# Layer 0's routing beside its attention, row transfers in pairs, layer 1's projection one period later, and VectorE's order there left to the scheduler

## The chip, the cores and the metric

The kernel runs on one core of one Trainium2 chip. The metric is device time in microseconds, the median of several runs: 1300.3 us for the kernel before (three runs, 1290.47 to 1302.03). Besides these there is one profiled execution, from which every detail below comes; its own time is given with the profile.

A core has engines that run independently and meet only through semaphores: TensorE (PE, with PEld for the loading of weights), VectorE (DVE), ScalarE (ACT), GpSimd (POOL) and SyncE (SP), whose queue issues most DMAs. [...]

## The reference

Four layers work on x of shape 4 x 512 x 128 (four batches of 512 tokens) with a context ctx of 4 x 154 x 128. Each layer adds an attention on the context and then a mixture of 8 experts, both on a layer norm of x:

```
x = x + attention_l(layernorm(x), ctx)
x = x + experts_l(layernorm(x))
```

Layer 0's attention is a similarity with softmax (H is the normalized x, C the context of the same batch):

```
Sim  = (H @ w1)[:, :, None] + (C @ w2)[:, None, :] + (H * w3) @ C.T + b
hq   = softmax(Sim, over C) @ C
hc   = softmax(max of Sim over C, over H) @ H         # one row per batch
out  = concat[H, hq, H * hq, H * hc] @ W_qv + b_qv
```

Layer 1's attention has 16 heads of 8 columns; queries, keys and values come from 8 x 8 matrices shared by all heads, there is a mask, and the output goes through Wo and bo. Layers 2 and 3 have 16 heads of 64 columns. The experts of layers 0, 2 and 3 take the best two of 8 experts for each token, those of layer 1 the best one with a capacity; layer 0's expert is a gated one with two up matrices, the others have one.

## The kernel before

**Tiling.** x stays in SBUF as four tiles x[b] of 128 x 4 x 128, one for each batch; a group of 128 tokens is a "tile" i of a batch. The experts of a layer run in two halves: half 0 holds the tokens of batches 0 and 1, half 1 those of batches 2 and 3. `route` (a generator, run in steps between its `yield`s) norms its two batches, computes the gate logits, finds the best experts, the rank of every token within its expert and from these a slot number (`su`, line 716). Scatters by indirect DMA from POOL's queue (line 721, one for 128 tokens and one choice) bring the normed tokens into blocks of 128 in DRAM, `buf`; `experts` loads these blocks (line 838, after all scatters of the half), runs up and down products, and stores `ybuf`; `gather` fetches the rows back by indirect DMA (line 939), and `combine` adds them to x (line 957). Scatters and gathers are first put into a list, `rows_due`; `row_transfers(n, behind)` issues the next n of them, tied with a wait to the instruction `behind`, or all at once without.

**Layer 0's attention** (`layer0_setup`, lines 960 to 1060). `prepare(b)` norms batch b, transposes it (xnT), and computes Sim for the four tiles in PSUM: a matmul with rhs1 (which holds w1 and w3 * C) and a second one, with w2b as its weights, that adds C @ w2 to every row (lines 979 and 980); VectorE copies to SBUF and adds b (line 983), takes maxima, and ScalarE exponentiates. `tile_of` divides by the sums, transposes the probabilities (pm and pt, copied by `evac`, which alternates between VectorE and ScalarE), multiplies by the context (hq), forms hc with its denominator by 4 + 4 matmuls with one column (lines 1034 and 1036), builds three feature tiles ft, and accumulates four products for each tile (line 1049). `attend_first` (from line 1261) runs `prepare(0)`, then tile(0), prepare(1), tile(1), prepare(2) and so on; layer 0's `route` for half 0 starts before prepare(3), goes six steps, and is finished after tile 3. After it, `row_transfers()` issues all its scatters, and `experts` begins. The buffer of sim exists once. No order is written by hand in layer 0; the framework's scheduler orders every engine's instructions by their place in the program and by a simulated timeline.

**Layer 1's attention** (`attend_all`, from line 1277). 16 periods, one for each tile of tokens, under `manual_schedule` for PE, ACT and DVE: on these engines instructions stay in the order in which the code writes them. A period overlaps the tile `new` (scores, maxima, exponentials) with the tile `old` before it (transposes, product with V, projection) and the first scores of `nxt`. The 16 heads are done in three groups g of 6, 6 and 4: `score(g)` on PE into a PSUM tile "sc" (two buffers), `most(g)` on VectorE (nm, line 291), `exp(g)` on ScalarE (line 305). `short` copies the last 26 columns of each head's probabilities; `inverse` takes the reciprocal of the sums; `replicate` transposes these (line 332), copies them (rT, line 334) and spreads them over 128 rows through DRAM by two DMAs of SP's queue (rd and rep, lines 339 and 340). `turn_ends`, `turn(0..3)` transpose old's probabilities into PSUM tiles "tr" (two buffers, also used by `replicate` and `project`); `take_ends`, `take(n)` copy these to SBUF on VectorE (line 261), and `take` also issues two row transfers; `by_v_ends`, `by_v(n)` multiply with V (line 405); `scaled` multiplies by rep (line 412); `project` (line 422) and `residual` (lines 1164 and 1165) add to x. `middle` and `after` run steps of `route` or of combining beside it, `parts` prepares the next batch (norm, values, keys and queries) in four portions. Before, a period of layer 1 (`narrow_period`, lines 432 to 485) is in this order:

```
new.score(1)  old.turn_ends  old.turn(0)  new.most(1)  new.exp(0)  new.exp(1)
old.take_ends  old.take(0)  old.by_v_ends  old.turn(1)  old.take(1)  new.score(2)
old.turn(2)  old.by_v(0)  old.by_v(1)  new.most(2)  new.exp(2)  old.take(2)
old.turn(3)  old.by_v(2)  old.take(3)  old.by_v(3)  old.scaled(0)
middle  parts  nxt.score(0)  nxt.most(0)  new.short  new.inverse  queries
new.replicate  old.project  old.residual  after
```

Layers 2 and 3 use `wide_period`, which stays as it is apart from an argument.

**The head of the program.** SP's queue issues x[0] to x[3], the two parts of the context (lines 108, 112, 113), then nine small loads for the gates (lines 1225, 1229, 183), then layer 0's weights (w_sim at line 207, then b_sim, b_qv, wqv), the clearing of `buf`, and layer 0's down matrices.

Of the kernel before, what the change touches and what calls it, by code (L numbers as in the profile page):

```python
# [19 lines left out]
P = 128  # L20
# [6 lines left out]
E = 8  # L27
# [19 lines left out]
def tile_xattn_moe_stack(ctx: ExitStack, tc: tile.TileContext, a: dict, out: bass.AP):  # L47
# [33 lines left out]
    turn = [0]  # L81

    def evac(o, i, scale=None):

        turn[0] += 1
        if turn[0] % 2:
            if scale is None:
                nc.vector.tensor_copy(o, i)
            else:
                nc.vector.tensor_scalar(o, i, scale, None, ALU.mult)  # L90
        elif scale is None:
            nc.scalar.copy(o, i)
        else:
            nc.scalar.activation(o, i, AF.Copy, scale=scale)
# [10 lines left out]
    x = []  # L105
    for b in range(B):
        t = xpool.tile([P, NI, D], F32, tag=f"x{b}", name=f"x{b}")
        nc.sync.dma_start(t, x_in[b])
        x.append(t)
# [3 lines left out]
    nc.sync.dma_start(ctail, a["ctx_1024"][:, P:S2, :].rearrange("b k d -> k b d"))  # L113

# [89 lines left out]
    def columns(src, rows, name):  # L204

        t = p2.tile([rows, P], F32, tag="rows", name=f"{name}_r")
        nc.sync.dma_start(t, src)
# [224 lines left out]
    def narrow_period(new, old, nxt=None, middle=nothing, queries=nothing, parts=nothing, after=nothing):  # L432
# [9 lines left out]
        if old:  # L442
            old.turn_ends()
            old.turn(0)
        if new:
            new.most(1)
            new.exp(0)
            new.exp(1)
        if old:
            old.take_ends("v")  # L450
            old.take(0, "v")
            old.by_v_ends()
            old.turn(1)
            old.take(1, "v")
        if new:
            new.score(2)
        if old:
            old.turn(2)
            old.by_v(0)
            old.by_v(1)  # L460
        if new:
            new.most(2)
            new.exp(2)
        if old:
            old.take(2, "v")
            old.turn(3)
            old.by_v(2)
            old.take(3, "v")
# [3 lines left out]
        parts()  # L472
        if nxt:
            nxt.score(0)
            nxt.most(0)
# [4 lines left out]
        if new:  # L480
            new.replicate()
        if old:
            old.project()
            old.residual()
        after()

    def wide_period(new, old, nxt=None, middle=nothing, queries=nothing, parts=nothing, after=nothing):
# [472 lines left out]
    def layer0_setup():  # L960
        wsim = columns(a["L0_xattn_w_sim"].rearrange("(k p) -> k p", p=P), 3, "wsim")
# [437 lines left out]
```

## Time and profile before

| | |
|---|---|
| median of three runs | 1300.3 us (1290.47 to 1302.03) |
| profiled execution, its own time | 1392.9 us |
| its span, first to last instruction | 1390.8 us |
| mean granted clock of TensorE | 0.902 |
| busy in the span: PE, DVE, ACT, POOL | 1125.7, 736.2, 575.6, 252.9 us |
| layer 0: attention, and the way to its experts | 0 to 117.6 us |
| layer 0: experts | 117.6 to 270 us |
| layer 1: attention (exponentials 271.2 to 519.4) | 271 to 521 us |
| layer 1: experts | 523 to 613 us |
| layer 2: attention, experts | 614 to 850, 855 to 978 us |
| layer 3: attention, experts and end | 979 to 1226, 1230 to 1391 us |

A profiled execution is one execution with the profiler on; its times of single instructions are read against its own total, not against the median. In lines of a timeline the columns are start and duration in us, engine, line of the kernel, operation, output and inputs, shapes, and count; in brackets the idle time of the engine ahead of it and what ended it. "remote" means that the profile knows no releaser on this core.

### The profile page before, as it was taken

The numbers are of one execution on the slowest core, as the hardware profiler recorded it, in microseconds if no ns is written. First come the engines' busy times: TensorE is split into PE (matmuls) and PEld (weight loads), VectorE is DVE, ScalarE is ACT, GpSimd is POOL, SyncE is SP. The second block draws the span as 40 slices with busy tenths as digits, with TensorE's granted clock in tenths as the row PEclk, the third lists the DMA queues.
The fourth block names the chain that finished last, engine by engine and source line by source line (L and its number), as shares of the span: only waits on it lengthen the run. The fifth ranks groups of instructions, "written<-read, shape, count | busy, mean of one in ns | idle before, by whom it ended". The sixth has DMA issues, their size and how long they took to land.

```text
span 1390.8 us, 26946 instructions
## 1 busy us (share of the span) xinstructions
PE 1125.7 (81%) x9435; PEld 924.2 (66%) x9435; DVE 736.2 (53%) x2057; ACT 575.6 (41%) x2290; POOL 252.9 (18%) x281
## 2 busy tenths in 40 slices
PE   5876998976777689788999988657879999898881
PEld 3766997833344348776878767646668778787771
DVE  4563546546667655235667665314456667454442
ACT  1113333543454444355665554212545655432220
POOL 2031314031000101302000031332220000304224
PEclk8787999968998879999999999767999999899996
DMA  6014685611010215532212224442321112245652
GB/s 210 1 65 118 207 251 182 196 51 29 9 22 27 70 27 141 148 98 47 47 32 56 54 66 121 120 124 80 116 47 39 40 33 47 66 109 142 179 163 69
DMA packets 136995, 126.80 MB, mean 91 GB/s; under 512 B 13466, under 2 KB 116511, under 8 KB 136479
## 3 DMA queue, kind: packets, MB, share of 16 engines
q1 hardware_dynamic: 129695, 110.39, 28.6%
q0 software_dynamic: 7168, 14.69, 3.7%
q8 instruction: 77, 1.26, 0.4%
q14 instruction: 55, 0.45, 0.1%
HBM read 101.31 MB, written 23.72 MB: 90 GB/s over the span
## 4 chain that ended last, share of the span: by engine, by line
PE 36%; DVE 8%; issue 4%; ACT 4%; DMA 4%; another core or an unknown queue 3%; POOL 1%; SPq 1%; POOLq 0%; DVEq 0%; ACTq 0%
PE sc L875 5%; PE sc L608 5%; PE av L405 4%; PE av L906 4%; PE tr L368 4%; PE tr L422 4%; DMA w<-in_up 3%; ACT probs L305 2%; PE sc L593 2%; PE av L387 2%; DVE nm L291 2%; PE sc L557 1%; POOL yg L939 1%; DVE aT L412 1%
## 5 line engine op out<-in xcount | busy, mean ns | idle before, releaser
L305 ACT ACTIVATE probs<-sc,nm 128x154 f32<-128x154 f32 x768 | 287.0, 402 | 193.6 <-DVE nm L291 178.4
L875 PE MATMUL sc<-tokT,w 128*128 128x128 f32 x1528 | 214.6, 290 | 19.8 <-DMA w<-in_up 14.8
L875 PEld LDWEIGHTS sc<-tokT,w 128*128 128x128 f32 x1528 | 195.0, 202 | 31.0 <-DMA w<-in_up 11.1
L906 PE MATMUL av<-w,hT 128*128 x1160 | 179.2, 292 | 42.7 <-issue 19.2
L291 DVE TENSOR_REDUCE nm<-sc 128x6 f32<-128x924 f32 x144 | 143.2, 1010 | 100.7 <-PE sc L608 47.9
L906 PEld LDWEIGHTS av<-w,hT 128*128 128x128 f32 x1160 | 155.9, 201 | 53.9 <-issue 22.9
L305 ACT ACTIVATION_READ_ACCUMULATOR probs<-sc,nm 128x1 f32 x768 | 168.0, 219 | 0.0
L939 POOL DMA_INDIRECT yg<-ybuf,su x112 | 107.0, 956 | 295.5 <-DVE ys L914 67.1
L233 POOL TENSOR_TENSOR rstd<-ve,nhalf 128x4 f32<-128x4 f32 x32 | 33.1, 1034 | 652.4 <-DVE ve L231 544.4
L721 POOL DMA_INDIRECT buf<-xn,su x112 | 108.4, 968 | 184.0 <-DVE eb L744 78.7
L261 DVE COPY pT<-tr 128x512 f32<-128x512 f32 x160 | 107.3, 687 | 62.0 <-PE tr L368 48.6
L368 PE MATMUL tr<-ident,probs 128*128 128x128 f32 x768 | 123.9, 293 | 0.7 <-DVE rT L334 0.7
L405 PE MATMUL av<-pT,vm 128*64 128x128 f32 (+1 forms) x1536 | 104.5, 285 | 18.4 <-DVE pT L261 16.8
L368 PEld LDWEIGHTS tr<-ident,probs 128*128 128x128 f32 x768 | 88.0, 148 | 29.4 <-issue 14.5
L914 DVE COPY ys<-av 128x128 f32<-128x128 f32 x168 | 48.0, 286 | 111.2 <-PE av L906 73.4
L405 PEld LDWEIGHTS av<-pT,vm 128*64 128x64 f32 (+1 forms) x1536 | 65.2, 127 | 46.8 <-DVE pT L261 25.9
L891 ACT ACTIVATE eg<-sc,w 128x128 f32<-128x128 f32 x184 | 52.9, 370 | 89.2 <-PE sc L875 52.2
L608 PE MATMUL sc<-kT,qT 64*128 64x154 f32 x1024 | 85.1, 304 | 3.5 <-ACT probs L305 3.5
L895 DVE SCALAR_TENSOR_TENSOR hT<-sc,w,eg 128x128 f32<-128x128 f32 x184 | 55.9, 342 | 53.4 <-ACT eg L891 50.6
L608 PEld LDWEIGHTS sc<-kT,qT 64*128 64x128 f32 x1024 | 69.8, 186 | 14.5 <-issue 10.1
L593 PE MATMUL sc<-xnT,wq 128*128 128x128 f32 x512 | 70.8, 296 | 2.9 <-ACT probs L305 2.9
L593 PEld LDWEIGHTS sc<-xnT,wq 128*128 128x128 f32 x512 | 64.9, 206 | 8.2 <-issue 4.3
(252 smaller groups left out, 1504.8 us busy)
## 6 DMA issues: line engine op xcount, KB each, us to landing
w<-in_up SPq DMA_DIRECT2D x46, 516.0 KB
w<-in_up SPq DMA_DIRECT2D x76, 258.0 KB
rep<-rd SPq DMA_DIRECT2D x64, 256.0 KB
ybuf<-ys SPq DMA_DIRECT2D x168, 64.0 KB
tok<-buf SPq DMA_DIRECT2D x36, 256.0 KB
w<-in_down SPq DMA_DIRECT2D x3, 2048.0 KB
w<-in_up SPq DMA_DIRECT2D x46, 128.0 KB
buf<-zero SPq DMA_DIRECT2D x2, 1472.0 KB
```

The lines of the kernel that those rows point to most:

```text
L261: return nc.vector.tensor_copy(o, i)
L291: nc.vector.tensor_reduce(self.at.heads(self.nm, g, n), self.sc[g][:, :, 0 : n * S2].rearrange("p j (s k) -> p j s k", s=n), AX.X, ALU.max ...
L305: nc.scalar.activation(self.pr[:, h, :], self.sc[g][:, j, s * S2 : (s + 1) * S2], AF.Exp, bias=self.nm[:, h : h + 1], accum_out=self.rs[:, ...
L368: nc.tensor.transpose(q[:, t * P : (t + 1) * P], self.pr[:, h, 0:P], ident)
L405: nc.tensor.matmul(av[rows, cols], v, self.pT[n][:, t, :], start=False, stop=last)
L593: nc.tensor.matmul(sc[:, c // 4, c % 4 * P : (c % 4 + 1) * P], wq[:, c * P : (c + 1) * P], at.xnT[:, i * P : (i + 1) * P], start=True, sto ...
L608: nc.tensor.matmul(sc[:, j, s * S2 : (s + 1) * S2], at.qT[i][rows, c, :], at.kT[rows, c, :], start=True, stop=True)
L721: ins = nc.gpsimd.indirect_dma_start(out=buf[half], out_offset=bass.IndirectOffsetOnAxis(ap=su[:, t : t + 1], axis=0), in_=xns[t // NI][:, ...
L875: nc.tensor.matmul(dst, w[:, at : at + P], xT, start=True, stop=True)
L895: products.append(nc.vector.scalar_tensor_tensor(hT[:, fc, :], up, b0, g, ALU.add, ALU.mult))
L906: nc.tensor.matmul(y[:, 0:D], hT[:, fc, :], w2[:, bass.ds(e, 1), fc, :].rearrange("p o d -> p (o d)"), start=(fc == 0), stop=(fc == nf - 1),)
L939: ins = nc.gpsimd.indirect_dma_start(out=yg[:, t, :], out_offset=None, in_=ybuf[half], in_offset=bass.IndirectOffsetOnAxis(ap=su[:, t : t ...
```

## The change

It has four parts.

- **Head and layer 0's arithmetic.** w_sim's rows and the context are loaded before x[1] to x[3]; the gates' small loads move behind layer 0's weights. C @ w2 + b is computed once for all batches (`row`) and added by VectorE when it takes Sim from PSUM, in place of the second matmul. The denominator of hc comes from one matmul on ScalarE's accumulated sum `es`. H * hc @ W3 + H @ W0 becomes one product with wc = W3 * hc + W0, so that three products are left of four.
- **Layer 0's order.** `sim` gets two buffers; batches 0 and 1 are prepared first, then tile 0, prepare(2), tile 1, three steps of `route`, prepare(3), five more (up to the list of scatters), tile 2, a step, tile 3. Four instructions of each tile call `row_transfers(2, ...)`.
- **Layer 1's period.** The order is new (below); the sums' reciprocals are replicated in the period after, and the projection and residual of a tile come two periods after its scores (`older`). Keys and queries use PSUM tiles "tr" and "av" instead of "sc". Transposed tiles that `evac` copies go to VectorE alone (`busy`).
- **VectorE in layer 1** is taken out of the engines whose order the code sets; the scheduler draws it up.

```diff
+    x = [xpool.tile([P, NI, D], F32, tag=f"x{b}", name=f"x{b}") for b in range(B)]
+    nc.sync.dma_start(x[0], x_in[0])
+    sim_rows = p2.tile([3, P], F32, tag="rows", name="sim_rows")
+    nc.sync.dma_start(sim_rows, a["L0_xattn_w_sim"].rearrange("(k p) -> k p", p=P))
...
+    for b in range(1, B):
+        nc.sync.dma_start(x[b], x_in[b])
```

The period of layer 1:

```diff
         if new:
             new.score(1)
-        if old:
-            old.turn_ends()
-            old.turn(0)
-        if new:
             new.most(1)
             new.exp(0)
-            new.exp(1)
+        if older:
+            older.project()
+            older.residual()
         if old:
+            old.replicate()
+            old.turn_ends()
             old.take_ends("v")
+            old.turn(0)
             old.take(0, "v")
             old.by_v_ends()
             old.turn(1)
             old.take(1, "v")
+        parts()
         if new:
+            new.exp(1)
             new.score(2)
-        if old:
-            old.turn(2)
-            old.by_v(0)
-            old.by_v(1)
-        if new:
             new.most(2)
             new.exp(2)
         if old:
+            old.by_v(0)
+            old.turn(2)
             old.take(2, "v")
+            old.by_v(1)
+        if nxt:
+            nxt.score(0)
+            nxt.most(0)
+        if old:
             old.turn(3)
+            old.take(3, "v")
             old.by_v(2)
-            old.take(3, "v")
             old.by_v(3)
             old.scaled(0)
         middle()
-        parts()
-        if nxt:
-            nxt.score(0)
-            nxt.most(0)
         if new:
             new.short()
             new.inverse()
         queries()
-        if new:
-            new.replicate()
-        if old:
-            old.project()
-            old.residual()
         after()
...
-    ordered = {mybir.EngineType.PE, mybir.EngineType.Activation, mybir.EngineType.DVE}
+    ordered = {mybir.EngineType.PE, mybir.EngineType.Activation}
+    ordered_all = ordered | {mybir.EngineType.DVE}
...
+        busy[0] = layer == 1
+        with tc.manual_schedule(engines=ordered if layer == 1 else ordered_all):
```

Layer 0:

```diff
+        row = w1.tile([P, B, S2], F32, tag="wv", name="row")
+        sc = ps_sc()
+        for j in range(2):
+            nc.tensor.matmul(
+                sc[:, j, 0 : 2 * S2],
+                w2b,
+                ctxT[:, 2 * j : 2 * j + 2, :].rearrange("p b k -> p (b k)"),
+                start=True,
+                stop=True,
+            )
+        nc.vector.tensor_scalar(
+            row.rearrange("p (j b) k -> p j (b k)", j=2), sc[:, :, 0 : 2 * S2], bsim, None, ALU.add
+        )
...
-            evac(pm, q)
+            row_transfers(2, evac(pm, q))
...
-            evac(pt, q[0:ST, :])
+            row_transfers(2, evac(pt, q[0:ST, :]))
...
+            wc = p2.tile([P, D], F32, tag="res1", name="wc")
+            nc.vector.scalar_tensor_tensor(wc, wqv[:, 3, :], hc, wqv[:, 0, :], ALU.mult, ALU.add)
+            ft = p2.tile([P, 2, S], F32, tag="vm", name="ft")
+            row_transfers(2, nc.scalar.copy(ft[:, 0, :], hq))
...
-                for k in range(4):
...
+                for k, (f, w) in enumerate(((ft[:, 0], wqv[:, 1]), (ft[:, 1], wqv[:, 2]), (xnT, wc))):
+                    nc.tensor.matmul(o[:, cols], f[:, cols], w, start=(k == 0), stop=(k == 2))
...
+            row_transfers(
+                2, nc.vector.tensor_tensor(t, o.rearrange("p (i d) -> p i d", i=NI), bc(bqv, 1, NI), ALU.add)
+            )
...
+        tiles = [prepare(b, found[b]) for b in range(2)]
+        tiles[0](0)
+        tiles.append(prepare(2, found[2]))
+        tiles[1](0)
+        beside = Steps(route(layer, 0, *gates[layer])).step(3)
+        tiles.append(prepare(3, found[3]))
+        beside.step(5)
+        tiles[2](0)
+        beside.step(1)
+        tiles[3](0)
         return beside.finish()
```

## The prediction

> **What bounds the kernel now.** I read the page, busy time by stage, then the timeline of the two stages touched. The page gives no single full engine (PE busy 81%, DVE 53%, ACT 41%), and its chain of waits falls apart into 1395 pieces, so stages are read. The fence below is the busy time by stage; columns: length, busy us and count of PE, PEld, DVE, ACT, POOL, granted clock, DMA share, GB/s.
>
> ```profile
> core 0: us, PE busy (x) PEld busy (x) DVE busy (x) ACT busy (x) POOL busy (x), PEclk, DMA share, GB/s
> 0.00:14.57 14.57, 3.00 (x13) 2.12 (x13) 11.03 (x65) 1.28 (x1) 8.63 (x29) 1.00 0.57 154
> 14.57:91.00 76.43, 65.17 (x354) 54.19 (x355) 42.81 (x157) 14.26 (x49) 3.02 (x3) 0.78 0.20 67
> 91.00:117.60 26.60, 6.54 (x47) 5.38 (x45) 6.91 (x27) 0.57 (x1) 16.63 (x17) 0.62 0.37 121
> 271.00:520.50 249.50, 183.66 (x1332) 96.41 (x1330) 150.67 (x338) 114.48 (x539) 28.08 (x29) 0.82 0.14 38
> ```
>
> The rows are the head, layer 0's attention, the handover to layer 0's experts, and layer 1's attention (16 periods). In the handover TensorE works 6.5 of 26.6 us while POOL is busy 16.6. In layer 1 nothing is full (PE 184, DVE 151, ACT 114 of 249.5), and the clock is 0.82 where layers 2 and 3 show 0.99 and 0.96 (their rows, 614 to 852 and 979 to 1228). The experts between (117.6 to 271) keep PE busy 95%; the change leaves them alone.
>
> The handover, from the timeline of all engines:
>
> ```profile
> 90.72 0.22 DVE L716 CAST su<-sl 128x8 uint32<-128x8 f32 x2
> ...
> 91.18 1.19 POOL L721 DMA_INDIRECT buf<-xn,su  x1 [8.46 <-DVE eb L744]
> ...
> 110.38 0.96 POOL L721 DMA_INDIRECT buf<-xn,su  x1 [0.30 <-issue]
> ...
> 112.77 5.28 SPq L838 DMA_DIRECT2D tok<-buf  x4
> ...
> 115.72 1.94 PE L848 MATMUL tr<-ident,tok 128*128 128x128 f32 x8 [15.59 <-DMA tok<-buf]
> ```
>
> The last slot number is cast at 90.9; 16 scatters then follow each other every 1.27 us until 111.3; only then may tokens be loaded, and TensorE has waited 15.6 us for them. So the experts' start (117.6) hangs on: x[1] final (64.9, the x add L1058) + 26.0 to the last slot + 20.3 of scatters + 6.3 of loads, transposes and a copy.
>
> Layer 1, the end of one period, same view:
>
> ```profile
> 405.45 0.55 ACT L316 COPY short<-probs 128x416 f32<-128x416 f32 x1
> ...
> 406.33 1.05 PE L1150 MATMUL sc<-kz,qT 64*128 64x462 f32 x4
> 407.42 1.12 DVE L291 TENSOR_REDUCE nm<-sc 128x6 f32<-128x924 f32 x1 [0.77 <-PE sc L1150]
> 408.46 0.24 DVE L327 RECIPROCAL rinv<-rs 128x16 f32<-128x16 f32 x1
> 408.58 0.39 ACT L305 ACTIVATE probs<-sc,nm 128x154 f32<-128x154 f32 x1 [2.58 <-DVE nm L291]
> ...
> 408.85 0.27 PE L332 MATMUL tr<-ident,rinv 128*16 128x128 f32 x1 [1.47 <-DVE rinv L327]
> ```
>
> ScalarE is through with the old tile at 406.0 and waits 2.58 us for the next maximum: next tile's score(0) runs only after by_v(3), the maximum after that; then the reciprocal must pass VectorE before TensorE (1.47 us idle) can transpose it, project, and start score(1). With the whole clock and nothing beside it a period takes 12.0 us (score(1) at 369.1 and 381.1). The mean from the first projection (303.2) to the fourteenth (511.4) is 208.2 / 13 = 16.0. Two causes of the 4 us difference, VectorE alone and then all engines:
>
> ```profile
> 417.55 0.29 DVE L412 TENSOR_TENSOR aT<-av,rep 128x128 f32<-128x128 f32 x1 [0.55 <-PE av L405]
> 417.75 0.86 DVE L224 BATCH_NORM_STATS2 st<-x 128x6 f32<-128x128 f32 x4
> ...
> 420.27 1.11 DVE L240 TENSOR_SCALAR xn<-x,mv,rstd 128x128 f32<-128x128 f32 x4
> ...
> 422.09 1.11 DVE L291 TENSOR_REDUCE nm<-sc 128x6 f32<-128x924 f32 x1
> ```
>
> 4.3 us of statistics, normalization and value tiles stand in VectorE's written order between the scaling and the maximum nm that ScalarE needs.
>
> ```profile
> 293.87 0.69 DVE L261 COPY pT<-tr 128x512 f32<-128x512 f32 x1 [2.56 <-remote]
> ...
> 297.05 0.95 POOL L939 DMA_INDIRECT yg<-ybuf,su  x1 [0.30 <-issue]
> 299.58 0.29 DVE L412 TENSOR_TENSOR aT<-av,rep 128x128 f32<-128x128 f32 x1 [5.02 <-PE sc L1150]
> ...
> 302.75 0.39 ACT L305 ACTIVATE probs<-sc,nm 128x154 f32<-128x154 f32 x1 [9.84 <-DVE nm L291]
> ```
>
> In a burst of eight row transfers VectorE stands 2.56 and 5.02 us although the transposes it needs were done, and ScalarE 9.84 behind it. The same shows at 319.2 (4.99) and 486.0 (4.47): 17 us for 24 transfers.
>
> **What the skill says.** "TensorE: Matmul & The Clock Gate", section "What's actually happening": an idle window of about 3.4 us halves TensorE's clock and a busy one restores it. The trace agrees: the clock's records change in multiples of 3.4 us, and matmuls of scores take twice the time at 33 us (0.26 apart) that they take at 69 us (0.13). "SBUF — State Buffer", section "Who interferes with whom": VectorE and GpSimd share a port pair that one instruction holds alone; this is a candidate for the stands above. The trace agrees only in part: other copies of the same shape ran their usual 0.68 us in the burst (290.6). "Perfetto Trace Analysis", section "Optimization Strategy": regimes with different limits gain from interleaving; the POOL-only handover beside an attention without scatters is such a pair.
>
> **Layer 0, part by part.** (1) The head. Today cm lands at 6.8 behind four x tiles, and wsim's rows are issued at 9.1 behind nine small loads; the first bias add is at 19.1. Moved to third and second in SP's queue, I estimate both by 4.5 (x[0], first, lands at 3.3, x[1] at 4.2); two transposes and copies (1.1 + 0.7 + 0.6 + 0.3), rhs1 (0.59), then the new row: w2b 0.28, two matmuls about 1.5 at half clock, one VectorE pass over 616 columns about 0.7, 1 us of handovers: first bias add near 11.5, 7 us earlier. The nine now queue behind wqv; their first reader is the routing, some 40 us later. (2) Matmuls, in instructions (two per fp32 matmul): w2b's, 8 a batch at 0.13 us (0.26 half clock); the sums of ebt, 6 of 8 at 0.12; the last product, 8 of 32 at 0.11 to 0.21. Together 2.6 to 4.5 us a batch, 10 to 18 for four, about half of it under VectorE. (3) VectorE: ft[2] (0.55) becomes hc (0.16) and wc (about 0.34); the bias add stays at two of 0.53. Nothing. (4) sim gets two buffers instead of one and two batches are prepared ahead. Today a batch ends every 14 to 17 us (x adds at 47.7, 64.2, 78.4, 93.2) with VectorE busy 25 of 40 us (42 to 82). VectorE's own work is about 10.5 us a batch (sum of its rows). From 11.5: 6.4 for the rest of tile 0, 8.5 for tile 1, 3.5 to prepare batch 2, and some 10 of PE latency not hidden: x[1] final near 42 instead of 64.9. (5) Routing stands ahead of tiles 2 and 3 instead of beside them; its bare chain, by its rows, is about 14 us, today 26: I take 20. Slots at 62. (6) The 16 scatters are tied to four evacuations each of tiles 2 and 3, two apiece, so the last pair also waits for tile 3's sum, which I put at 75 to 80. Back to back they end at 62 + 20.3 = 82.3; loads 6.3: experts start at 88.6. The stands of layer 1 (17 us per 24) would be up to 11 us for 16; none shows beside today's scatters, where VectorE has nothing to do. Bounds 0 and 11, I take 5. Start at 94 against 117.6: **24 us gained**; bounds 12 (26 for routing as today, 11 of stands) and 34 (tile 3's sum at 75, + 2.5 + 6.3).
>
> **Layer 1.** New period, whole clock, 0 at score(1), with durations of the period at 369: score(1) to 1.55, nm(1) 1.6 to 2.7. The older tile's projection and the old rinv's transpose are done by 2.0, but each holds one of two "tr" banks until VectorE, busy with nm(1), has read it (3.0 and 3.5). turn_ends 3.0, turn(0) 3.55; tails and pT0 copied by 5.0; by_v_ends 4.35, turn(1) 4.8, score(2) 5.2 to 6.4; by_v(0), turn(2), by_v(1) to 7.7; next score(0) 7.7 to 9.25; turn(3), by_v(2) to 10.1; VectorE takes nm(0) 9.3 to 10.4, then pT3 to 11.1; by_v(3) ends 11.5. **11.5 against 12.0: 0.5 x 16 = 8 us.** nm(0) is done 1 us before the period ends, so exp(0) no longer waits on the critical path. replicate's two DMAs (2.0 and 1.5 to land, 4.1 with issue) follow rT at 3.5 and are there near 8, before scaled at 11.6; today they have a similar 8 us. Cover is 3.5 us: a load of layer 2's weights that blocks SP (up to 8.1 us once) uses it up, three times at most, and then the next period's projection is late. Keys and queries leave the score banks and come before score(2); today that period is 14.7, 2.7 longer, of which about 1.5 stays (the 1.44 us kz pass): 1.2 x 3 = 4 us. VectorE's 4.3 us of other work (and routing steps) may now fall into the 3.5 us a period that it is free; I take 1.5 us in five periods: 7 us. Four evacuations leave ScalarE (0.58) for VectorE (0.68): under 1 us each, hidden by the same free time. The stands beside bursts stay. Tail: one more period without new scores, beside experts that keep TensorE busy; nothing. **Sum 19 us**, bounds -20 (an order that costs 1.25 us a period) and 40 (half the stands and 13 us of clock on top).
>
> **Sum.** The profiled execution took 1392.9 (span 1390.8). 1392.9 - 24 - 19 = 1349.9. The median of the runs stands at 1300.3 / 1392.9 = 0.9335 of it; scaled, **1260 us**.
>
> **Rivals.** *Layer 0 only* (0.18): today's 4 us over 12.0 may be half clock and bursts, which no order removes: (1392.9 - 24) x 0.9335 = 1278. For it: 0.5 us a period is little. Against: the 4.3 us of filler ahead of nm is plain. *More* (0.14): fewer idle windows bring layer 1's clock toward the 0.99 of layer 2; half clock covers 18% x 2 of 249 us, and a sixth of that back, 15 us more: 1392.9 - 58 gives 1246. *Slower* (0.10): VectorE's order in layer 1 is drawn from supposed durations with whole clock, while TensorE's and ScalarE's are fixed by hand. Where the drawn order puts a copy or sum that waits for late TensorE work ahead of nm, VectorE stands, and ScalarE, then the score banks behind it. Its price in one place is the stand already seen, 5 us; in each of 16 periods 80: 1392.9 - 24 + 80 gives 1353. It cancels layer 0's gain at 24 / 16 = 1.5 us a period. Against: an order by readiness seldom puts long waits first. *Scatters not hidden* (0.08): the burst stands and tile 3's late sum leave 10 of layer 0's 24: 1392.9 - 10 - 19 gives 1273.
>
> **How the numbers follow.** Likeliest (0.50): 1260, its own range 1240 to 1277. Measurement tells about 1% here, 1287 to 1313 being no change. Faster: 0.49 + 0.13 + 0.14 + 0.06 = 0.82; same 0.10 (of layer 0 only 0.05, scatters 0.02, slower 0.02, likeliest 0.01); slower 0.08. Range 1232 to 1292: it leaves out the slower case and the tip of the better one, under 0.2.
>
> **What would show it.** Layer 0: first bias add near 11.5; scatters starting before 70 while tiles 2 and 3 run; experts' first up matmul near 94, not 117.6. Layer 1: score(1) to score(1) 11.5 in a bare period; ScalarE's waits for nm down from today's 100 us (27.5 + 42.8 + 30.1 in its three stretches); span of its exponentials 230 against 248. Wrong if the slots come after 75, if VectorE's stands grow with the paced scatters, or if VectorE waits at its head while nm is ready.

## The result and the profile after

The changed kernel takes **1285.8 us** (median of 20 runs, 1277.49 to 1296.07); the kernel before, beside it, 1298.6 (20 runs, 1290.47 to 1306.88). The ratio is **0.9904, interval 0.9883 to 0.9925**: 12.8 us faster, where 40 were forecast.

The profile of before that the prediction read (1392.9 us) has the level of a chip on which this kernel takes 1391 us (median of 27 runs, in the experiments below); the medians here come from chips on which it takes 1297 to 1303. So the kernel before was profiled again on one of the latter (1305.15 us, span 1303.0), and that profile is the one compared here. The profiled executions of this document lie up to 12 us from the medians of their kernels; the changed kernel's own (1280.46, span 1278.7) lies 5 below. Medians therefore decide, and profiles say where.

Busy time by stage, columns as in the prediction's first fence. First the kernel before on the faster chip: head to the first bias add, layer 0 to the last slot, handover, layer 1's attention.

```profile
0.00:19.00 19.00, 7.47 (x29) 6.21 (x29) 11.25 (x66) 1.28 (x1) 8.61 (x29) 1.00 0.69 190
19.00:91.20 72.20, 60.80 (x337) 50.21 (x338) 42.57 (x156) 14.25 (x49) 3.02 (x3) 0.76 0.16 52
91.20:117.80 26.60, 6.56 (x46) 5.46 (x45) 6.90 (x27) 0.57 (x1) 16.61 (x17) 0.63 0.36 121
266.30:492.40 226.10, 171.69 (x1345) 92.35 (x1344) 152.15 (x346) 114.86 (x539) 28.21 (x29) 0.89 0.16 42
```

The same four of the changed kernel:

```profile
0.00:18.00 18.00, 7.82 (x27) 5.95 (x28) 12.12 (x67) 1.28 (x1) 8.43 (x29) 1.00 0.70 193
18.00:73.30 55.30, 37.38 (x178) 29.64 (x176) 33.95 (x128) 12.51 (x46) 2.01 (x2) 0.69 0.21 70
73.30:104.20 30.90, 21.65 (x124) 16.71 (x124) 15.82 (x61) 2.92 (x8) 18.68 (x18) 0.77 0.32 105
253.60:471.40 217.80, 171.40 (x1339) 88.29 (x1339) 149.75 (x338) 112.60 (x534) 28.30 (x29) 0.91 0.16 44
```

The slots come 18 us earlier and the scatters now run beside TensorE (21.65 us busy in the handover instead of 6.56), but the handover is 4.3 us longer, and the head is 1 us shorter, not 7. Layer 1's stage loses 8.3 us, and its experts gain 3.4 back (87.9 to 91.3). VectorE's stands beside bursts of row transfers are gone in both. In the profile of before that the prediction read, waits with a releaser that the profile doesn't know are led by these two (columns: waiting tile, total us, times, longest):

```profile
DVE ys L914 <- remote: 29.7, 8, 8.9
ACT hT L884 <- remote: 29.3, 6, 7.4
```

All of them sum to 113 us, 110 of these on VectorE and ScalarE. 79 us are at ys, hT and eg, which belong to the experts; aT and pT, where the prediction saw its stands in attention, have 20.7. So most of them are no matter of attention's bursts. On the faster chips no profile shows one.

The handover of the changed kernel, from the timeline:

```profile
73.08 0.22 DVE L714 CAST su<-sl 128x8 uint32<-128x8 f32 x2
...
73.54 1.19 POOL L719 DMA_INDIRECT buf<-xn,su  x1 [15.71 <-DVE eb L742]
...
95.20 1.34 POOL L719 DMA_INDIRECT buf<-xn,su  x1 [2.24 <-DVE res L1065]
...
102.04 1.11 PE L846 MATMUL tr<-ident,tok 128*128 128x128 f32 x4 [7.02 <-DMA tok<-buf]
```

Scatters start at 73.5. Fourteen follow one another until 91.8; the last pair is tied to tile 3's sum (L1065), and GpSimd stands 2.24 us for it. (L846 is the first transpose of the experts' tokens.)

### The profile page after: what moved, and what is told of

It reads as the page before. It is cut to its first block, busy times and chain, and to the rows that moved or that the text cites. A ratio compares the mean times of both kernels' runs of the same rounds, so it can differ in the third digit from the quotient of the medians.

```text
span 1278.7 us, 26797 instructions
## 1 busy us (share of the span) xinstructions
PE 1086.2 (85%) x9351; PEld 890.2 (70%) x9351; DVE 738.7 (58%) x2066; ACT 574.5 (45%) x2290; POOL 253.1 (20%) x281
## 4 chain that ended last, share of the span: by engine, by line
PE 56%; DVE 13%; DMA 12%; issue 7%; ACT 5%; POOL 4%; SPq 2%; POOLq 0%; DVEq 0%; ACTq 0%
PE sc L873 9%; PE tr L370 6%; PE av L904 6%; PE av L407 5%; PE sc L606 5%; DMA w<-in_up 5%; PE tr L424 5%; ACT probs L307 3%; PE sc L591 3%; DVE nm L293 3%; DMA yg<-ybuf,su 3%; POOL yg L937 2%; PE av L389 2%; PE sc L1159 2%; PE tr L357 2%
## 5 line engine op out<-in xcount | busy, mean ns | idle before, releaser
L873 PE MATMUL sc<-tokT,w 128*128 128x128 f32 x1528 | 211.7, 286 | 22.2 <-DMA w<-in_up 17.4
L873 PEld LDWEIGHTS sc<-tokT,w 128*128 128x128 f32 x1528 | 190.6, 198 | 35.6 <-DMA w<-in_up 11.4
L904 PE MATMUL av<-w,hT 128*128 x1160 | 168.5, 281 | 4.8 <-DVE hT L893 3.0
L937 POOL DMA_INDIRECT yg<-ybuf,su x112 | 106.4, 950 | 255.7 <-DMA rd<-rT 61.3
L904 PEld LDWEIGHTS av<-w,hT 128*128 128x128 f32 x1160 | 148.3, 194 | 11.7 <-DVE hT L893 4.1
L263 DVE COPY pT<-tr 128x512 f32<-128x512 f32 x160 | 107.0, 684 | 43.6 <-PE tr L370 37.7
L370 PEld LDWEIGHTS tr<-ident,probs 128*128 128x128 f32 x768 | 84.9, 144 | 33.4 <-issue 21.6
L889 ACT ACTIVATE eg<-sc,w 128x128 f32<-128x128 f32 x184 | 53.2, 368 | 87.5 <-PE sc L873 77.5
```

Of the source, the lines that this page charges most:

```text
L263: return nc.vector.tensor_copy(o, i)
L370: nc.tensor.transpose(q[:, t * P : (t + 1) * P], self.pr[:, h, 0:P], ident)
L873: nc.tensor.matmul(dst, w[:, at : at + P], xT, start=True, stop=True)
L904: nc.tensor.matmul(y[:, 0:D], hT[:, fc, :], w2[:, bass.ds(e, 1), fc, :].rearrange("p o d -> p (o d)"), start=(fc == 0), stop=(fc == nf - 1),)
L937: ins = nc.gpsimd.indirect_dma_start(out=yg[:, t, :], out_offset=None, in_=ybuf[half], in_offset=bass.IndirectOffsetOnAxis(ap=su[:, t : t ...
```

## The experiments

Stages are given as three lengths in us, layer 0's attention with the way to its experts / layer 1's attention / layer 1's experts, each to the first scores or up products of the next stage (within 0.5 us). Ratios (with 95% intervals) compare with the kernel before on the same chip. An order of VectorE is "written" where the code sets it and "drawn" where the scheduler does.

**The chip, and the two halves of the change (a chip where before takes 1391 us).** First the kernel before unchanged:

> The kernel before, unchanged, for a second profile. The profiled execution shown before took 1392.9 us where its median is 1298.6, and four stages that the change does not touch are together some 60 us longer in it than in the profile after. Theory 1: that one execution was disturbed; here the span is near 1298, the waits whose releaser is unknown (110 us in all) are gone, layer 1's attention takes 225 to 232 us instead of 248, and layer 0's experts start near 115. Theory 2: the old profile is typical of profiled executions of this kernel: span again near 1390, with the same waits beside row transfers.

1397.17 us, span 1395.0, with 96 us of waits with unknown releaser: the level goes with the chip, as 27 runs there with a median of 1391.2 say, too. Why that chip has these waits is not known. Then head and layer 0 alone:

> The kernel before with the change's head and layer 0 alone (early rows and context, row added by VectorE, three products, two sim buffers, routing ahead of tiles 2 and 3, paired scatters). Theory 1 (the gain is layer 0's): 9 to 13 us less than before, ratio 0.990 to 0.993. Theory 2 (the gain is layer 1's): under 4 us, ratio over 0.997. My prediction had 24 us here.

0.9952 (0.9931 to 0.9973), 6.7 us. Layer 1's part alone:

> The kernel before with the change's layer 1 alone (new period, later projection, VectorE's order drawn up by the scheduler, copies on VectorE). Theory 1 (the gain is layer 0's): within 3 us of before, ratio 0.998 to 1.002. Theory 2 (the gain is layer 1's): 9 to 19 us less, ratio 0.986 to 0.993. Theory 3 (the drawn order costs): slower, ratio over 1.003.

0.9851 (0.9820 to 0.9883), 21 us. The changed kernel with VectorE's order in layer 1 written again:

```diff
-        with tc.manual_schedule(engines=ordered if layer == 1 else ordered_all):
+        with tc.manual_schedule(engines=ordered_all):
```

> The changed kernel, with VectorE put back among the engines whose order the code sets in layer 1. If the drawn order is what holds layer 1's gain down, this is faster than the changed kernel by 5 us or more: ratio to before under 0.987. If the drawn order fills VectorE's free time as I supposed, it is slower by 5 us or more: ratio over 0.994. Between them the order of VectorE does not matter, as the maxima are limited by TensorE and the banks.

0.9912 (0.9880 to 0.9944): the new period without the drawn order keeps 0.4 percentage points beside layer 0's 0.5 (the intervals overlap). Here layer 1's part looked like the gain. But the unknown waits also fell, from 96 us to 75 in the run with layer 1's part, so about all of its 21 us could be fewer of them (with layer 0's part alone they were 103). The halves had to be run again where there are none.

**The kernel before on a faster chip, the changed kernel, and the drawn order by itself.**

> The kernel before once more, for a profile beside the next runs. Theory 1 (the level depends on the chip): its span agrees within 1.5% with the median of the runs of before in this call, whichever level that has, and if the level is near 1299, no wait has an unknown releaser, layer 1's attention takes 225 to 232 us, and layers 2 and 3 take what they take in the profile after (229 and 236 us). Theory 2 (a single execution can be disturbed): the span differs from the median by over 3%.

> The changed kernel itself. If this is a chip of the 1391 us kind and the two parts add up as measured (0.9952 and 0.9851), the ratio to before is 0.978 to 0.983; if it is of the 1299 us kind, 0.988 to 0.993 as in the result. If the parts disturb each other, over 0.985 on the first kind.

1305.15 for the one; 0.9877 (0.9831 to 0.9924) for the other, stages 107.0 / 215.6 / 94.1 against 117.8 / 226.1 / 87.9. Then one line of the kernel before:

```diff
-        with tc.manual_schedule(engines=ordered):
+        with tc.manual_schedule(engines=ordered - {mybir.EngineType.DVE} if layer == 1 else ordered):
```

> The kernel before with one edit: in layer 1 VectorE is taken out of the engines with a written order. Theory 1 (VectorE's filler work standing ahead of the maxima is most of what layer 1 lost): ratio 0.987 to 0.993. Theory 2 (the new period with its later replication and projection is what counts, the drawn order helps only with it): ratio over 0.996.

0.9881 (0.9831 to 0.9930); layer 1 at 210.6 / 89.9, shorter than in the changed kernel. One line brings as much as the whole change. And four row transfers at each of layer 0's places instead of two:

```diff
-            row_transfers(2, evac(pm, q))
+            row_transfers(4, evac(pm, q))
```

(and so at the other three)

> The changed kernel with four row transfers instead of two at each of the four places of layer 0's tile, so that all 16 scatters are released by tile 2 and none waits for tile 3's sum. If that wait is what held layer 0's gain down, the scatters run back to back from the last slot (near 74), end near 95, and the experts start 3 us (chip of the 1299 kind) to 8 us (1391 kind) earlier than in the changed kernel, with the ratio to before lower by 0.003 to 0.006. If the scatters hold VectorE up, tile 3 ends later and nothing is gained.

0.9838 (0.9799 to 0.9878). Twelve scatters now follow one another; the last four stand 2.42 us for tile 2's sum. All 16 take 22.7 us instead of 24.3 and 26.8 in the changed kernel's two profiles, and the experts start at 103.1 instead of 104.2 and 107.0: by the profiles, pacing them to tile 3's sum cost 1 to 4 us. The interval of the ratio overlaps the changed kernel's.

**Joining, and three suspects (another faster chip).** The changed layer 0 with fours, beside the old period with the drawn order:

> The changed layer 0 with four row transfers at each of its places, and layer 1 with the period of before, but VectorE's order drawn. Theory A (the two gains are separate; the new period only costs): layer 0's stage about 103, layer 1's about 211, its experts 88 to 90, so 15 + 15 us off the kernel before: ratio 0.975 to 0.979, below every kernel so far. Theory B (the gains overlap, because what layer 0 gains is given back at the waits after it, or the new period is needed): no better than the four transfers alone, ratio 0.984 to 0.988.

1272.79 us, **0.9795** (0.9746 to 0.9844), stages 101.4 / 217.5 / 88.6. The lowest ratio so far, just above Theory A's 0.975 to 0.979; its interval overlaps that of the fours. But layer 1 took 217.5 and not 211. Its code there is that of the kernel before with the drawn order, yet the traces show VectorE's instructions in another order (32 stretches of some 366 instructions differ), and the span from the first to the last of the 16 third-group maxima is 205.9 instead of 198.9. So the same code can be drawn in different orders.

```diff
-    found = {b: stats(x[b]) for b in range(B)}
+    found = {b: stats(x[b]) for b in range(2)}
```

(and the other two after tile 0)

> The changed kernel, but the statistics of batches 2 and 3 are written after tile 0 and not in the head. Theory A (these 8 statistics and their small operations stand in VectorE's queue ahead of rhs1 and xn and hold the head): first bias add 3 us or more earlier than 18.0 (near 15), x[1] final near 52 instead of 55.4, experts' first up matmul near 101, ratio 0.997 to 0.998 of the changed kernel, that is 0.986 or so of the kernel before. Theory B (the head waits for the loads of the context and TensorE at half clock, not for VectorE): first bias add still at 17 to 18, time as the changed kernel's (0.988 to 0.990).

0.9869 (0.9831 to 0.9907), first bias add 17.6. The edit did not move what it meant to: the scheduler pulled all 16 statistics ahead of rhs1 again. As VectorE's order in layer 1 is the changed kernel's, it serves as the changed kernel's time on this chip.

```diff
-        parts()
         if new:
             new.exp(1)
+        parts()
+        if new:
             new.score(2)
```

> The changed kernel, but in layer 1's period exp(1) stands ahead of the parts (keys, queries, routing) in ScalarE's and TensorE's written orders. Theory A (the qT copies that wait in ScalarE's queue ahead of exp(1), 27.5 + 11.7 + 3 us in the changed kernel's layer 1, hold the period): ScalarE's waits at the qT copy fall below 15 us and layer 1's stage shortens by 3 us or more, from 216 to 218 down to 213; ratio 0.985 to 0.987. Theory B (that wait lies inside one for the score banks or VectorE and only moves): stage 215 to 219, ratio 0.988 to 0.991.

0.9868 (0.9829 to 0.9906), equal to the run ahead of it. ScalarE's waits at the qT copy fell from 27.5 to 9.2 us, those for nm rose from 76.8 to 90.0: the wait moved (Theory B). Stage (213.4) and ratio are what A expected, but the changed kernel itself has this ratio here, so no gain shows.

```diff
-        if older:
-            older.project()
-            older.residual()
...
             old.take(1, "v")
+        if older:
+            older.project()
+            older.residual()
```

> The changed kernel, but the older tile's projection and residual stand after the value products of the old tile's first quarter, not ahead of its last transposes. Theory A (the new period's cost is that turn_ends waits for a tr bank that the older tile's residual frees only after nm(1), 16.8 us in all by the trace): TensorE's waits at the transposes for the residual fall to 3 us or less, the bare period comes near 10.8 as in the kernel before with VectorE's order drawn, and the stage shortens by 4 to 6 us to 211 to 213: ratio 0.983 to 0.986. Theory B (the bank is only one of several things late in the period): stage 215 to 219, ratio 0.988 to 0.991.

0.9873 (0.9835 to 0.9910), stage 219.6, a little above B's. TensorE's 16.8 us of waits for the residual are gone, and nothing is gained: Theory B.

**The head with its order fixed, and layer 1's halves without unknown waits (a third faster chip).** VectorE's order of the head written by hand:

```diff
-    prepare = setups[0]()
-    found = {b: stats(x[b]) for b in range(B)}
+    with tc.manual_schedule(engines={mybir.EngineType.DVE}):
+        found = {0: stats(x[0])}
+        prepare = setups[0]()
+        first = [prepare(0, found[0])]
+        found[1] = stats(x[1])
+        first.append(prepare(1, found[1]))
+        found.update({b: stats(x[b]) for b in range(2, B)})
```

(with the new row's add behind xnT)

> The changed kernel, but VectorE's order in the head is written by hand: statistics of batch 0 first, then the context's copies, rhs1, w2b, xn, xnT, the new row, batch 0's similarity, and only then the statistics of batches 1, 2 and 3. (Writing two of them later in the program, as the run of that name did, moved none of them: 16 statistics still stood ahead of rhs1.) Theory A (12 statistics of later batches ahead of rhs1 and xn, some 3.5 us, hold the head): rhs1 at about 9.5 instead of 12.6, first bias add at 14.5 (plus or minus 0.7) instead of 18.0, and x[1] final at 52 to 53 instead of 55.4; experts' first up matmul near 101, and 2 to 4 us off the kernel. Theory B (later steps wait for TensorE or for what the loads bring): first bias add earlier, but x[1] final stays at 55 to 56 and the time as the changed kernel's, 0.987 to 0.990.

0.9928 (0.9903 to 0.9952). rhs1 at 8.2 instead of 12.6, first bias add at 15.6 instead of 18.0; x[0] final at 42.7 and x[1] at 57.1 (41.3 and 55.4 in the changed kernel). The statistics do hold the head, but this earlier head arrives nowhere: Theory B, and a little slower than that. The written order also puts batch 1's similarity at 27.4 instead of 20.5, and its work then stands in tile 0's way (below). The same head in the joined kernel:

> The joined kernel (changed layer 0 with four transfers at each place, layer 1's old period with VectorE's order drawn) with that head. Theory A: first bias add 14.5, experts' first up matmul near 99 instead of 101.4, ratio 0.977 to 0.979. Theory B: 0.979 to 0.981, as the joined kernel. What the drawn order of layer 1 happens to be moves both by up to 7 us: the same code in layer 1 was drawn in two different orders in two kernels, and the span of its maxima was 198.9 and 205.9.

1271.86 us, 0.9835 (0.9786 to 0.9885), x[1] again at 55.4, stages 103.3 / 210.4 / 87.5: above what both theories had, and not to be told from the joined kernel (the intervals overlap). Layer 1's third-group maxima span 198.8 us here with an order that differs from the joined kernel's in 20 stretches only, and one and the same order spans 198.9 and 201.4 in the two runs of the drawn order alone; so the 7 us of the joined kernel can't be put down to the draw alone. Then layer 1's part alone, and the drawn order alone:

> Layer 1's part alone (new period, later projection, keys and queries in other banks, drawn order of VectorE), beside the old layer 0. Only its difference to the next run counts. Theory A (the new period is worth nothing beside the drawn order, and its tail costs 3 us): slower than the next run by 3 to 8 us. Theory B (the new period brings the 4 us of keys and 8 us of bare periods that were forecast): faster by 5 us or more. Theory C (they can't be told apart, the draw decides): within 3 us. Third-group maxima from first to last: 203 to 207 here.

> The kernel before with one edit, VectorE's order in layer 1 drawn. Ratio 0.986 to 0.990 as in its first run; third-group maxima from first to last 199 to 200, layer 1's stage 210 to 212, its experts 88 to 90. Beside the run ahead of it: under Theory A lower by 3 to 8 us, under B higher by 5, under C within 3.

**1.0006** (0.9982 to 1.0029) against **0.9928** (0.9907 to 0.9949), medians 1297.08 and 1286.06 (22 runs each). The new period with its late projection undoes what the drawn order brings: 11 us apart, Theory A and more than its 3 to 8. The two kernels differ in the period, the banks of keys and queries, and the copies given to VectorE; these were not tried one by one. Layer 1's attention and its experts, first with layer 1's part, then with the drawn order alone:

```profile
262.20:480.90 218.70, 171.55 (x1340) 86.77 (x1339) 149.82 (x338) 112.40 (x534) 28.32 (x29) 0.91 0.16 44
480.90:572.20 91.30, 83.19 (x668) 75.67 (x670) 33.94 (x120) 41.96 (x134) 18.42 (x19) 0.94 0.49 134
```

```profile
266.20:479.30 213.10, 167.01 (x1345) 88.03 (x1344) 148.66 (x339) 114.24 (x539) 28.53 (x29) 0.91 0.16 45
479.30:566.10 86.80, 78.08 (x663) 71.89 (x665) 32.60 (x115) 41.68 (x133) 18.47 (x19) 0.98 0.51 140
```

5.6 us lie in the periods and 4.5 in the experts behind. The clock is 0.91 in both attentions, so it does not explain the former; in the experts it is 0.94 against 0.98. Third-group maximum to maximum, four periods that are at full clock in both kernels (the 6th, 7th, 10th and 15th) take 10.9, 12.5, 10.9, 11.4 with the new period and 10.5, 10.8, 10.5, 10.4 with the old. The 6th, first new, then old:

```profile
340.76 0.80 DVE L291 TENSOR_REDUCE nm<-sc 128x4 f32<-128x616 f32 x1
...
351.71 0.80 DVE L291 TENSOR_REDUCE nm<-sc 128x4 f32<-128x616 f32 x1
```

```profile
348.12 0.80 DVE L291 TENSOR_REDUCE nm<-sc 128x4 f32<-128x616 f32 x1
...
358.58 0.80 DVE L291 TENSOR_REDUCE nm<-sc 128x4 f32<-128x616 f32 x1 [0.30 <-PE sc L1150]
```

**Layer 0's part alone and the whole change on one faster chip.**

> Head and layer 0 of the change alone, layer 1 as before. Only its difference to the next run, the whole change on the same chip, counts. Theory A (layer 1's part is worth nothing, so the whole gain is layer 0's): ratio 0.988 to 0.992, and within 4 us of the next run. Theory B (layer 1's part is worth the 8 to 10 us by which its stage was shorter in the changed kernel's trace): slower than the next run by 7 us or more, ratio 0.995 to 0.998.

> The changed kernel unchanged, beside layer 0's part alone. Ratio 0.988 to 0.991 under both theories; under A within 4 us of the run ahead of it, under B faster than it by 7 us or more.

0.9872 (0.9829 to 0.9915) and 0.9870 (0.9826 to 0.9914), medians 1284.16 and 1284.72: Theory A. Layer 0's part alone is as fast as the whole change (each ratio is known to about 0.004, some 6 us).

## Why the prediction was wrong

The direction held, and the time lies within the range (1232 to 1292), but the gain is 12.8 us where the likeliest case had 40. Both sums failed: layer 0's at the head and at what follows it up to x[1], layer 1's at the 12.0 us from which it counted the old period.

**The scale.** "The stands of layer 1 (17 us per 24)" were taken for a cost of row transfers. They are the other chip's: beside the same burst in the kernel before on a faster chip (transfers from 282 us on) VectorE stands at most 0.76 us up to 299 us. The Trainium skill, "SBUF — State Buffer", section "Who interferes with whom", gave the prediction its candidate, a port pair that VectorE and GpSimd share; no run here shows it at work. The ratio 0.9335 scaled all work down, although the difference goes with a block of waits that one chip adds. It changes the sum little (43 to 40), but a 249.5 us stage that is 226.1 elsewhere made layer 1's slack look larger than it is.

**Layer 0, forecast 24, measured about 10.** The experts' start is at 116.5 on average over four profiles with the old layer 0 on the faster chips (117.8, 119.0, 112.9, 116.2) and at 106.4 over seven with the new one and pairs (104.2, 107.0, 103.9, 107.5, 104.4, 109.4, 108.1). By the run of layer 0's part alone it is 11 to 22 us (0.9829 to 0.9915), of which the profiles don't show more than these 10. In the changed kernel's own profile the start is at 104.2 and not at 94: x[1] is 13.4 us late, routing 2 us quicker, the scatters 4 us longer, and the 5 us for stands are not needed. (The upper bound of 34 could not be: with slots at 62 the prediction's own start is 88.6 without any stand, a gain of 29.)

- *Step 1, the head, failed.* The first bias add is at 18.0, not 11.5. The loads did come earlier: the context's transposes start at 6.1 instead of 7.9. But VectorE has all 16 statistics of the four batches ahead of rhs1, which comes at 12.6.

```profile
10.56 0.83 DVE L226 BATCH_NORM_STATS2 st<-x 128x6 f32<-128x128 f32 x4
...
12.62 0.57 DVE L966 TENSOR_SCALAR rhs<-ctxT,wsim 128x616 f32<-128x616 f32 x1
...
17.96 0.48 DVE L993 TENSOR_TENSOR sim<-sc,row 128x308 f32<-128x308 f32 x1 [1.19 <-PE sc L990]
```

  The prediction counted the six steps of its chain and none that the scheduler could put between. With the order fixed the add is at 15.6, still 4 behind the forecast (the new row's matmuls and the scores' take 2.4 us each there, one after the other, with batch 0's transposes between; the forecast had 1.5 for the first and nothing for the second).
- *Step 4, x[1] at 42, failed.* It is final at 55.4. Half of the 13.4 us is the head's (6.5); the rest is the stretch from the first bias add to x[1], 37.4 us against 30.5 forecast (the parts named there sum to 28.4, which would have put x[1] at 39.9). In the kernel before, on the faster chip, it takes 46.1. "6.4 for the rest of tile 0" was a sum of VectorE's rows; tile 0 takes 23 us (18.0 to 41.3), in which TensorE and ScalarE take their turns between VectorE's steps. TensorE is at half clock from 24.9 to 38.5 (the 512-column product takes 1.96 and 2.07 us, 1.02 at 41.2). The Trainium skill, "TensorE: Matmul & The Clock Gate", section "What's actually happening", has half clock after an idle window of about 3.4 us; here the trace agrees only in part, as TensorE is busy 1.21 of the 3.4 us ahead. Two small loads of later layers' set-up, queued on SP behind layer 0's down matrix, stand in this chain, too: the mask (mi, for layer 1's madd) and gate (for layer 2).

```profile
29.16 0.16 DVE L1036 COPY mall<-tr 128x1 f32<-128x1 f32 x1
30.57 0.48 DVE L1106 TENSOR_SCALAR madd<-mi 128x616 bf16<-128x616 int32 x1 [1.25 <-DMA mi<-in_mask_Bx1xSxS_if]
30.97 0.23 DVE L1038 TENSOR_SCALAR md<-sm,mall 128x4 f32<-128x4 f32 x1
31.00 0.20 ACT L1199 ACTIVATE gate<-gate 128x1 f32<-128x1 f32 x1 [1.48 <-DMA gate<-in_L_xattn_gate]
...
31.23 0.20 ACT L1041 ACTIVATE ebt<-md 128x4 f32<-128x4 f32 x1
```

  Batch 0's md has its inputs at 29.3 and runs at 31.0, behind madd, which waits for its load; ebt follows md. The Trainium skill, "PSUM — Partial Sum Buffer", section "Engine vs sequencer instructions", says that the queues of ScalarE and VectorE are strict FIFO (first in, first out), and the trace agrees. The loads cost tile 0 at most 1.6 us (ebt at 31.23 instead of some 29.6), and no run moved them. With the head's order fixed nothing waits for them, and ebt comes no earlier all the same:

```profile
30.88 0.20 DVE L1040 TENSOR_SCALAR md<-sm,mall 128x4 f32<-128x4 f32 x1
...
31.86 0.19 ACT L1201 ACTIVATE gate<-gate 128x1 f32<-128x1 f32 x1
31.95 0.20 ACT L1043 ACTIVATE ebt<-md 128x4 f32<-128x4 f32 x1
```

  There batch 1's scores run on TensorE (25.3 to 27.3) ahead of batch 0's second product with the context, and batch 1's four exponentials on ScalarE (30.2 to 31.9) ahead of gate and ebt, which is ready at 31.1. So the head's 2.4 us are gone before tile 0 ends. Whether an earlier head helps with batch 1's work elsewhere was not tried.
- *Step 5, routing 20, was right:* 18 us (55.4 to 73.3). The slots' place, 62, fails only by x[1].
- *Step 6:* one scatter each 1.27 us as forecast, but 24.3 us in all (24.1 to 29.3 over the seven profiles), since tile 3's sum comes at 94.9 (94.23 + 0.68), not at 75 to 80. Loads and transposes 6.4 (6.3 forecast). No 5 us of stands.
- *Step 2* had 10 to 18 us less TensorE work. Up to the experts' start TensorE is busy 66.9 us instead of 74.8 (the rows of the stages above), 8 less. *Step 3*, "nothing" for VectorE, held: 61.9 against 60.7. Which of layer 0's edits brings its gain was not tried one by one.

**Layer 1, forecast 19, measured 0 (within about 3 us beside the old layer 0, some 8 beside the new).** The drawn order brings 9 to 16 us, and the new period takes some 11 of them back.

- *"11.5 against 12.0" failed, by its second number.* The new period is as forecast: 10.9 to 12.5, mean 11.4 in the four periods above. But 12.0 was no property of the old order of TensorE and ScalarE; it came from VectorE's written order. With that drawn (the only edit) the old period takes 10.5, and so it does in all four profiles that have it. The step credited the new period with what the drawn order gives, and the new one is 0.9 longer. What makes it longer is open: the wait behind the residual's bank (16.8 us) went in one run and most of the one behind qT (27.5 to 9.2) in another, and the time stayed both times. The new period with a written order was not run on a faster chip.
- *Keys, 1.2 x 3 = 4 us, don't show.* The new period makes the next batch's keys in the 3rd, 7th and 11th period, the old one in the 4th, 8th and 12th. The nine periods that cover both (3rd to 5th, 7th to 9th, 11th to 13th) sum to 131.6 us with the new period and to 121.7 with the old one, both drawn (127.9 to 131.6 over five profiles on the faster chips with the new period, 120.7 to 133.3 over four with the old).
- *Filler, 7 us, was the right mechanism and undersized:* the drawn order alone brings those 9 to 16 us (0.9928 and 0.9881), the bare periods' 1.5 us among them. It is also uneven. In the changed kernel's third period, which takes 19.9 us, the scores of the next tile are done at 293.8, and nm follows only at 297.3, behind combines that wait for gathered rows: in one place, the rival "slower".

```profile
292.74 1.05 PE L1159 MATMUL sc<-kz,qT 64*128 64x462 f32 x4
...
296.74 0.35 DVE L955 SCALAR_TENSOR_TENSOR x<-yg,wb,x 128x128 f32<-128x128 f32 x1 [0.98 <-DMA yg<-ybuf,su]
...
297.34 1.10 DVE L293 TENSOR_REDUCE nm<-sc 128x6 f32<-128x924 f32 x1
```

  These 3.5 us are a part of what this period is longer; the keys and a clock of 0.83 fall into it, too.
- *Tail, "nothing", failed:* on the faster chips layer 1's experts take 91.3 to 94.1 in five profiles with the whole change or layer 1's part, 87.9 and 89.7 with layer 1 as before. One more projection and residual now come into them; how much of the 3.5 us is theirs, and how much the clock's (0.94 against 0.98 above), was not tried.

ScalarE's waits for nm in the stage fell from 87.3 to 76.8 us. The profiles together leave layer 1's part a gain of some 5 us (8.8 less in the attention, 3.5 more in the experts), the medians none. The distance of single executions from their medians, up to 12 us, covers that; it isn't settled further. Nor is the 21 us that layer 1's part brought on the slower chip, beyond the fall in unknown waits.

**The rivals.** "Layer 0 only" is what happened, with about half of its layer 0: 1278 was its time, 1286 came. "Scatters not hidden" applied to 1 to 4 us. "More" did not happen. The chances put 0.5 on a sum of two gains each of which had been read from one profile. That the measured time lies in the range is luck: two errors of the same sign, with the rival's 1278 inside the range, too.

## What to carry to other kernels

Before a shorter period is credited to a new order on one engine, let the others' order go free in the old period first: the baseline may be set by the order of an engine that the edit doesn't mean. An order drawn by a scheduler can differ between kernels with the same code in that place, so measure it in each kernel, and look where an engine's late waits stand ahead of what others need. And an edit that shortens one link of a chain (head, slots) is worth only what the next link lets through: here another batch's work in the same queues, set-up loads that land at 31 us, and a last transfer tied to the last tile.

## What was not expected of the hardware

- Two levels of chip: the kernel before takes 1391 us on one and 1297 to 1303 on the others. Its traces tell them apart: 96 and 110 us of waits of VectorE and ScalarE with unknown releaser, up to 8.9 us each, in the two profiles with the longer time, none in the one with the shorter.
- An edit's gain differs with that level: layer 1's part 0.9851 (0.9820 to 0.9883) on the slower and 1.0006 (0.9982 to 1.0029) on a faster one, layer 0's part 0.9952 (0.9931 to 0.9973) and 0.9872 (0.9829 to 0.9915).
- The best version here, the joined one: 1272.79 and, with the fixed head, 1271.86 us, 0.9795 (0.9746 to 0.9844) and 0.9835 (0.9786 to 0.9885), against 0.9904 for the change.
